# A bidirectional recurrence with slot attention on one core: its denominators get three buffers of their own, and the first four gates are taken in two steps

## The chip, the cores and the metric

The kernel runs on one core of one Trainium2 chip. A core has five engines with an instruction stream each: PE (matrix products and transposes), DVE (vector operations), ACT (activation functions from tables, copies), POOL (vector operations too) and SP, which here issues most of the DMA transfers; ACT issues some. They meet only at semaphores. The metric is the device time of one launch in microseconds, the median of several runs: 1080.36 us before the change (five runs, 1079.99 to 1083.6).

## The reference

`x` is 4 x 1024 x 1024 (batch, tokens, features), `fside` has the same shape and `cond` is 4 x 256. First a recurrence runs over the tokens, forward and backward, for each of the 4 x 1024 pairs of batch and feature on its own. `fside` is both the key and the value, `x` goes through a sigmoid as a gate:

```python
tf = sigmoid(sum(time_emb, -1))
decay = exp(-exp(w)) * (0.5 + 0.5 * tf)
ek = exp(min(k, 30.0)); ekv = ek * v
# scan over tokens: a = a * decay + ekv_t ; b = b * decay + ek_t   (forward: nf, df; reversed: nb, db)
euk = exp(min(u + k, 30.0))
num = nf + nb - ekv + euk * v
den = df + db - ek + euk
out = sigmoid(r) * (num / max(den, 1e-08)) * (0.8 + 0.2 * tf)
```

Its result passes two blocks of a slot attention: logits of each token against 16 slots, the four best tokens of each slot written into it, 16 heads of attention of all tokens over the 16 slots, an output projection and a normalisation by the root of the mean square. At the end `x` is added. All is float32.

## The kernel before

**The recurrence** takes the first 400 us or so. Features lie on the 128 partitions and tokens along them, so that one *tile* is 128 features of one batch by 1024 tokens. There are N = 32 tiles, eight per batch; the loop over `i` begins at line 587. Every four tiles share one buffer of gates (`HK` = 4).

What one tile `i` goes through, by engine:

- SP loads the keys (`kf`, four buffers) and, four tiles at a time, the gates' input (`load_gates`, L273, four transfers into one buffer of 4 x 1024 columns).
- ACT: exponentials of the keys (`terms_exp`, L292; `own_exp`, L315), the edge values that carry a forward sum into the backward scan (`make_edge`, L344, one for the denominator and one for the numerator), a matrix with the decay on its diagonal (`decay_matrix`, L382), and the first guess of the quotient, Ln and then Exp of the denominator (`guess`, L426 and L428). Also copies out of PSUM and the Square of the output (L468).
- POOL: clamping and `ekv` (`terms`, L302, L308); the floor of the denominator (L405); denominator times guess and gate times guess (`gated`, L441, L442); gate times the corrected factor (`product`, L465).
- DVE: forward scans of `ek` and `ekv`, backward scan of the denominator (`scan`, L323), the token's own term added to the denominator (`den_sum`, L352), a Newton step on the quotient (`newton`, L452), the own term of the numerator (`own_value`, L365), and the backward scan of the numerator over pairs of tokens (`numerator`, L411).
- PE: sums for the numerator (`make_pairs`, `add_pairs`), the products for the logits and sums of squares (`contract`, L476), transposes of the output rows (L493), and preparations of weights.

The order is written out by hand: `pin` (L78) keeps the instructions of each engine in the order of the program text. The tiles overlap: while tile `i` is in its scans, tile `i-1` gets its quotient and tile `i-2` its rows. In round `i` POOL's order is L441 and L442 of tile `i-1`, L302 and L308 of tile `i+1`, L405 of tile `i`, L465 of tile `i-1`. DVE's order is the two forward scans and the backward scan of tile `i`, L352 of tile `i`, L452 of tile `i-1`, L365 and L411 of tile `i`. ACT ends a round with `guess` of tile `i` and the exponential of tile `i+2`.

**The sigmoids** are taken for four tiles at once at the head of every fourth round (`gates`, L278, called at L605). The sigmoid and the pair of Exp and Ln lie in different table sets of ACT, so that each call of `gates` has a table load before it (shown at L279) and one after it (L177). Rounds with `i % HK == 0` take a branch of their own (L596 to L609): they have no transposes of rows, first PE's sums, then on ACT the Square, `own_exp`, the first edge, the sigmoids, the second edge. All other rounds take the branch from L610, with rows of tile `i-2` turned and copied between those steps.

**The buffers.** Denominator and numerator of a tile lie in one buffer, `both`, of 2 x 1024 columns and two more, of which one holds the numerator's edge. There are two such buffers, so the first write of tile `i` (the forward scan of `ek` at L323) waits until the last reader of tile `i-2` is done. For the denominator's part that is POOL's product L465, which stands at the end of round `i-1`. The other rotating buffers named below are `ek`, `ekv` and `quo`, two each. After the loop a tile `raw_sb` with a buffer of its own (tag `ov`) and `stage_last` (tag `both`) are used for the logits and the last rows.

**After the recurrence** come the two blocks, in which PE is busy nearly all the time. The change does not touch them.

Of the kernel before, what the change touches and what calls it, by code (L numbers as in the profile page):

```python
# [10 lines left out]
F32 = mybir.dt.float32  # L11
U32 = mybir.dt.uint32
AF = mybir.ActivationFunctionType
# [5 lines left out]
P = 128  # L19
# [19 lines left out]
def kernel(  # L39
# [25 lines left out]
    nc = tc.nc  # L65
# [193 lines left out]
    with rec_stack:  # L259
# [15 lines left out]
            for k in range(HK):  # L275
                move(gate[n][:, k, :], xt[n // 2, ts(n % 2 * HK + k, P), :])

        def gates(n):  # L278
            pin(nc.scalar.activation(gate[n], gate[n], AF.Sigmoid))  # L279
            pin(load_exp_ln())  # L280

        def gate_of(i):
# [44 lines left out]

        def sums(i, ek, ekv, parts):

            flat = rec.tile([P, 2 * L + 2], F32, tag="both", bufs=2, name=f"both_{i}")  # L330
            both = flat[:, : 2 * L].rearrange("p (n t) -> p n t", n=2)
            for n, src in enumerate((ek, ekv)):
                dst = both[:, n, :]
                for part in parts:
                    at = part.start
                    scan(
                        dst[:, part], src[:, part], i, dst[:, at - 1 : at] if at else 0.0, False
                    )
            return flat, both, [edges[:, i % 8, :], flat[:, 2 * L : 2 * L + 1]]

        def make_edge(i, both, edge, n):

            b, k = i // NK, i % NK
            pin(nc.scalar.mul(edge[n], both[:, n, L - 1 : L], turn[:, b, k : k + 1]))  # L344

        def denominator(i, both, edge):
            den = both[:, 0, :]
            scan(den, den, i, edge[0], True)

        def den_sum(both, own):  # L350
            den = both[:, 0, :]
            pin(nc.vector.scalar_tensor_tensor(den, own, EXP_CLAMP, den, ALU.min, ALU.add))  # L352


# [28 lines left out]
            return m  # L383

        def make_pairs(i, both, by):
            f = both[:, 1, :].rearrange("p (s h) -> p h s", h=2)
            pairs = rec_ps.tile([P, 4, P], F32, tag="ptr", bufs=1, name=f"pairs_{i}")
            pairs = pairs.rearrange("p q c -> p (q c)")
            pin(nc.tensor.matmul(pairs, by, f[:, 1], start=True, stop=False))
            pin(nc.tensor.matmul(pairs, ident, f[:, 0], start=False, stop=True))  # L390
            return pairs

        def add_pairs(num_ps, flat, by):

            f = flat[:, L : 2 * L].rearrange("p (s h) -> p h s", h=2)
            later = flat[:, L + 2 :].rearrange("p (s h) -> p h s", h=2)[:, 0]
            return [
                lambda: add(num_ps, 0, f[:, 0]),
                lambda: add(num_ps, 1, f[:, 1]),
                lambda: add(num_ps, 1, later, by),  # L400
            ]

        def floor(both):
            den = both[:, 0, :]
            pin(nc.gpsimd.tensor_scalar(den, den, DEN_MAX, DEN_MIN, ALU.min, ALU.max))  # L405

        def numerator(i, both, edge, pairs):
            even = both[:, 1, :].rearrange("p (s h) -> p h s", h=2)[:, 0]
            dec = decay_2[:, i // NK, i % NK : i % NK + 1].to_broadcast([P, L // 2])
            pin(  # L410
                nc.vector.tensor_tensor_scan(  # L411
                    even[:, ::-1], dec, pairs[:, ::-1], edge[1], ALU.mult, ALU.add
                )
            )

        def numerator_half(i, both, edge, h):

            num = both[:, 1, ts(h, 512)]
            scan(num, num, i, edge[1] if h else both[:, 1, 512:513], True)

        def guess(i, both, parts=(every,)):

            quo = rec.tile([P, L], F32, tag="quo", bufs=2, name=f"quo_{i}")
            b = i // NK
            for part in parts:
                pin(nc.scalar.activation(quo[:, part], both[:, 0, part], AF.Ln))  # L426
                pin(
                    nc.scalar.activation(  # L428
                        quo[:, part],
                        quo[:, part],  # L430
                        AF.Exp,
                        scale=-1.0,
                        bias=half_log_gain[:, b : b + 1],
                    )
                )
            return quo

        def gated(i, both, quo, part=every):
            xk = gate_of(i)[:, part]
            den = both[:, 0, part]  # L440
            pin(nc.gpsimd.tensor_tensor(den, den, quo[:, part], ALU.mult))  # L441
            pin(nc.gpsimd.tensor_tensor(xk, xk, quo[:, part], ALU.mult))  # L442

        def newton(i, both, quo, num_ps, part=every, out=None):

            b = i // NK
            den = both[:, 0, part]
            num = num_ps[:, part]
            if out is None:
                den, num = parted(den, i), by_half(num)  # L450
            pin(
                nc.vector.scalar_tensor_tensor(  # L452
                    den if out is None else out[:, part],
                    den,
                    twice_root[:, b : b + 1],
                    num,
                    ALU.subtract,
                    ALU.mult,
                    reverse0=True,
                )  # L460
            )
# [125 lines left out]
        for i in range(N):  # L587
# [5 lines left out]
            flat[i], both[i], edge[i] = sums(i, ek[i], ekv[i], [every] if past else halves)  # L593

            adds = add_pairs(num_ps[i - 1], flat[i - 1], by[i - 1]) if past else [lambda: None] * 3
            if i % HK == 0:  # L596
                for fill in adds:
                    fill()
                if older:
                    square(i - 2, quo[i - 2])  # L600
                own_exp(i, kf[i], own[i])
                make_edge(i, both[i], edge[i], 0)
                if i == 0:
                    make_edge(i, both[i], edge[i], 1)
                gates(i // HK)  # L605
                if past:
                    make_edge(i, both[i], edge[i], 1)
                    late_stage = staged(i - 2)
                    contract(i - 2, quo[i - 2], NK)  # L609
            else:  # L610
                blocks = []
                if older:
                    stage = staged(i - 2)
                    blocks = [rows_block(i - 2, h, stage) for h in range(2)]
                if i > HK and i % HK > 1:
                    blocks.append(rows_block(i - i % HK - 2, i % HK - 2, late_stage))
                if i >= 3 and projection:
                    blocks.append(projection.pop(0))
                blocks = blocks[:2] + [None] * (4 - len(blocks)) + blocks[2:]
                copy = [None] * 4  # L620

                def turn_block(n):
                    copy[n] = blocks[n]() if blocks[n] else lambda: None

                turn_block(0)
                adds[0]()
                copy[0]()
                if older:
                    square(i - 2, quo[i - 2])
                adds[1]()  # L630
                make_edge(i, both[i], edge[i], 0)
                turn_block(1)
                adds[2]()
                copy[1]()
                own_exp(i, kf[i], own[i])
                turn_block(2)
                if older:
                    contract(i - 2, quo[i - 2], NK, (0,))
                copy[2]()
                make_edge(i, both[i], edge[i], 1)  # L640
                turn_block(3)
                if older:
                    contract(i - 2, quo[i - 2], NK, (1,))
                copy[3]()
# [32 lines left out]
            floor(both[i])  # L677
            if past:
                newton(i - 1, both[i - 1], quo[i - 1], num_ps[i - 1])
                product(i - 1, both[i - 1][:, 0, :], nc.gpsimd)  # L680
                store_turned(i - 1)
            num_ps[i] = own_value(i, kf[i], own[i])
            if i == N - 1:
# [11 lines left out]

        i = N - 1
        halves = [(h, ts(h, 512)) for h in (1, 0)]
        raw_sb = rec.tile([P, L], F32, tag="ov", bufs=1, name="raw_sb")
        sq = rec_ps.tile([P, L], F32, tag="own", bufs=1, name="sq")
        eps_col = rc.tile([P, 1], F32, name="eps_col")  # L700
        nc.gpsimd.memset(eps_col, EPS)
# [7 lines left out]
        for n, (h, part) in enumerate(halves):  # L709
            numerator_half(i, both[i], edge[i], h)  # L710
            gated(i, both[i], quo[i], part)
            add(num_ps[i], h, both[i][:, 1, part])
            if n == 0:
                contract_half(i - 1, False, h)
        contract_half(i - 1, True, 1)
# [54 lines left out]
        for n in range(4):  # L770
            for q in range(4):
                block = gate_of(i - 1 + n // 2)[:, ts(4 * (n % 2) + q, P)]
                pin(nc.tensor.transpose(banks[n][:, q, :], block, ident))
        stage_last = rec.tile([P, 2 * L + 2], F32, tag="both", bufs=2, name="stage_last")[:, :L]
        stage_last = stage_last.rearrange("p (t c) -> p t c", c=P)
        for j, stage in ((i - 1, staged(i - 1)), (i, stage_last)):
            for h in range(2):
# [663 lines left out]
```

## Time and profile before

| | |
|---|---|
| median of five runs | 1080.36 us (1079.99 to 1083.6) |
| profiled execution, its own time | 1079.68 us |
| its span | 1077.3 us |
| mean granted clock of PE | 0.987 |
| busy: PE, DVE, POOL, ACT | 985.9, 739.4, 548.5, 516.2 us |
| 100 to 350 us: DVE busy in each 50 us | 48.34 to 48.83 us |
| 100 to 350 us: POOL busy in each 50 us | 48.60 to 48.94 us |
| 447 us to the end: PE busy | 613.55 of 630.30 us |

The span runs from the first to the last instruction on the core; the execution's own time has 2.4 us more around it. A busy time counts the instructions of one engine, with overlaps between two that follow each other counted once. In a row of the timeline the first number is the start in us from the span's start, the second the duration, and the brackets tell for how long the engine stood idle before and what ended that. In the chain of work the columns are start, length and what the end hung on at that time. Tile names are those of the program without numbers; `both` is the buffer of denominator and numerator.

### The profile page before, as it was taken

The numbers are of one execution on the slowest core, as the hardware profiler recorded it, in microseconds if no ns is written. First come the engines' busy times: TensorE is split into PE (matmuls) and PEld (weight loads), VectorE is DVE, ScalarE is ACT, GpSimd is POOL, SyncE is SP. The second block draws the span as 40 slices with busy tenths as digits, with TensorE's granted clock in tenths as the row PEclk, the third lists the DMA queues.
The fourth block names the chain that finished last, engine by engine and source line by source line (L and its number), as shares of the span: only waits on it lengthen the run. The fifth ranks groups of instructions, "written<-read, shape, count | busy, mean of one in ns | idle before, by whom it ended". The sixth has DMA issues, their size and how long they took to land.

```text
span 1077.3 us, 12290 instructions
## 1 busy us (share of the span) xinstructions
PE 985.9 (92%) x4232; PEld 548.1 (51%) x4232; DVE 739.4 (69%) x1049; ACT 516.2 (48%) x818; POOL 548.5 (51%) x417
## 2 busy tenths in 40 slices
PE   4688898888889888999999999998999999999996
PEld 1223333232323324665666666664575767767663
DVE  7899999999999974244666565665244555555555
ACT  6586877878687742123333444444023333333332
POOL 4999999999999961001222222222001444444344
PEclk9899999999999999999999999999999999999999
DMA  8585474758655273951777786554750555555554
GB/s 276 163 306 159 163 240 144 251 175 271 186 168 166 88 247 105 368 221 64 254 269 252 275 282 245 196 176 166 284 205 21 195 182 209 195 212 191 193 206 156
DMA packets 121790, 218.81 MB, mean 203 GB/s; under 512 B 10928, under 2 KB 76592, under 8 KB 121728
## 3 DMA queue, kind: packets, MB, share of 16 engines
q1 hardware_dynamic: 87872, 199.15, 52.6%
q10 hardware_dynamic: 33280, 16.78, 5.4%
q0 software_dynamic: 576, 2.10, 0.5%
q8 instruction: 33, 0.54, 0.2%
q14 instruction: 29, 0.24, 0.1%
HBM read 150.90 MB, written 67.11 MB: 202 GB/s over the span
## 4 chain that ended last, share of the span: by engine, by line
PE 60%; POOL 18%; ACT 9%; issue 7%; DVE 3%; DMA 1%; SPq 1%; POOLq 0%; ACTq 0%; DVEq 0%
PE psc L1170 21%; PE po L1227 19%; POOL gate L442 4%; POOL ekv L308 4%; POOL gate L465 3%; PE ptr L1158 3%; PE pk L1030 3%; PE pkv L960 3%; PE pv L1098 2%; POOL both L405 2%; POOL ek L302 2%; POOL both L441 2%; ACT quo L428 2%; ACT quo L426 1%; PE pet L1216 1%
## 5 line engine op out<-in xcount | busy, mean ns | idle before, releaser
L1170 PE MATMUL psc<-km,xt 128*128 128x272 f32 (+1 forms) x1024 | 238.4, 386 | 0.0
L1227 PE MATMUL po<-vm,e 128*128 128x512 f32 x512 | 230.4, 593 | 0.9 <-ACT e L1217 0.9
L1170 PEld LDWEIGHTS psc<-km,xt 128*128 128x128 f32 x1024 | 189.5, 190 | 29.1
L1204 POOL TENSOR_TENSOR e<-e,den 128x256 f32<-128x256 f32 x64 | 40.6, 635 | 252.4 <-DVE den L1202 231.3
L1227 PEld LDWEIGHTS po<-vm,e 128*128 128x128 f32 x512 | 94.8, 190 | 95.7 <-issue 84.9
L1268 DVE SCALAR_TENSOR_TENSOR y<-y,inv,npost_bc 128x1024 f32<-128x1024 f32 x62 | 79.6, 1284 | 41.3 <-POOL inv L1263 41.3
L1236 DVE TENSOR_TENSOR y<-po,y 128x512 f32<-128x512 f32 x128 | 85.9, 674 | 30.2 <-PE po L1227 29.9
L1256 ACT ACTIVATE junk<-y 128x1024 f32<-128x1024 f32 x63 | 66.7, 1059 | 69.3 <-DVE y L1268 69.1
L1263 POOL TENSOR_TENSOR inv<-mean,minus_half 128x1 f32<-128x1 f32 x64 | 35.6, 557 | 96.8 <-DVE mean L1261 96.8
L441 POOL TENSOR_TENSOR both<-both,quo 128x1024 f32<-128x1024 f32 (+1 forms) x33 | 77.0, 2334 | 11.0 <-ACT quo L428 9.5
L373 PE MATMUL num<-both,ident 128*128 128x512 f32 x128 | 68.8, 660 | 10.1 <-DVE both L411 6.8
L308 POOL TENSOR_TENSOR ekv<-ek,kf 128x1024 f32<-128x1024 f32 (+1 forms) x33 | 76.4, 2315 | 2.6
L1217 ACT COPY e<-pet 128x256 f32<-128x256 f32 x64 | 23.8, 372 | 112.4 <-PE pet L1216 112.3
L323 DVE TENSOR_TENSOR_SCAN both<-columns,ek 128x1024 f32<-128x1024 f32 (+1 forms) x32 | 72.2, 2255 | 7.9 <-POOL gate L465 6.5
L442 POOL TENSOR_TENSOR gate<-gate,quo 128x1024 f32<-128x1024 f32 (+1 forms) x33 | 76.2, 2308 | 0.0
L323 DVE TENSOR_TENSOR_SCAN both<-columns,edges,both 128x1024 f32<-128x1024 f32 x32 | 74.4, 2325 | 1.7 <-ACT edges L344 1.7
L1365 POOL TENSOR_TENSOR y<-y,xin 128x1024 f32<-128x1024 f32 x31 | 73.2, 2360 | 1.4 <-DVE y L1268 1.4
L465 POOL TENSOR_TENSOR gate<-gate,both 128x1024 f32<-128x1024 f32 x31 | 73.5, 2372 | 0.3
L323 DVE TENSOR_TENSOR_SCAN both<-columns,ekv 128x1024 f32<-128x1024 f32 (+1 forms) x32 | 71.4, 2231 | 0.0
L1161 ACT COPY xt<-ptr 128x512 f32<-128x512 f32 x64 | 36.9, 577 | 69.3 <-PE ptr L1158 69.3
L1261 DVE TENSOR_SCALAR mean<-total 128x1 f32<-128x1 f32 x64 | 9.8, 154 | 85.8 <-ACT junk L1256 45.8
L476 PE MATMUL raw<-quo,lhs 128*32 128x512 f32 x128 | 65.3, 602 | 0.0
(214 smaller groups left out, 1638.8 us busy)
## 6 DMA issues: line engine op xcount, KB each, us to landing
y<-rows SPq DMA_DIRECT2D x64, 512.0 KB, 4.3
kf<-in_ft_dram SPq DMA_DIRECT2D x32, 512.0 KB, 5.2
gate<-in_xt_dram SPq DMA_DIRECT2D x32, 512.0 KB, 7.6
turned_rows<-gate SPq DMA_DIRECT2D x32, 512.0 KB, 3.5
xt<-turned_rows SPq DMA_DIRECT2D x32, 512.0 KB, 5.6
rows<-y SPq DMA_DIRECT2D x32, 512.0 KB, 3.0
xin<-in_x_dram SPq DMA_DIRECT2D x32, 512.0 KB, 4.6
rows<-stage ACTq DMA_DIRECT2D x31, 512.0 KB, 3.7
```

What stands on the lines that cost most here:

```text
L308: pin(nc.gpsimd.tensor_tensor(ekv[:, part], ek[:, part], kf[:, part], ALU.mult))
L323: nc.vector.tensor_tensor_scan(dst[:, way], dec, src[:, way], start, ALU.mult, ALU.add)
L373: nc.tensor.matmul(num_ps[:, ts(h, 512)], by, src, start=False, stop=True, skip_group_check=True)
L441: pin(nc.gpsimd.tensor_tensor(den, den, quo[:, part], ALU.mult))
L442: pin(nc.gpsimd.tensor_tensor(xk, xk, quo[:, part], ALU.mult))
L465: pin(engine.tensor_tensor(xk, xk, factor[:, part], ALU.mult))
L1170: nc.tensor.matmul(psc[g][:, :n], xt_g[g][:, k, :], maps["km"][:, g // NT, k, :n], start=(k == 0), stop=(k == NK - 1),)
L1227: nc.tensor.matmul(po, et[:, ts(c, P)], vm[:, c, ts(h, 512)], start=(c == 0), stop=(c == 1),)
L1236: pin(nc.vector.tensor_add(half, po, half))
L1256: pin(nc.scalar.activation(junk, src, AF.Square, accum_out=total))
L1268: pin(nc.vector.scalar_tensor_tensor(y[g], y[g], inv[g], npost_bc, ALU.mult, ALU.mult))
L1365: pin(nc.gpsimd.tensor_add(y[g - 1], y[g - 1], xin[g - 1]))
```

## The change

It has three parts.

1. Each denominator gets a buffer of its own, `den`, of which there are three. The numerator and its edge stay in a buffer `num_sb` of 1024 + 2 columns, two of them. `both` becomes a list of the two, and the functions that took a slice of the old tile take an element of the list.
2. `gates` is called with the tile's number. At tile 0 it takes the sigmoid of feature tile 0 only, at tile 1 that of the feature tiles 1 to 3; at tiles 4, 8, ... that of all four as before. Tile 1 therefore takes the branch that the fourth tiles take; the square and the contraction in it are now only done where there is a tile `i-2`.
3. `raw_sb` moves into a buffer of `ekv`, and `stage_last` into one of `num_sb`. The space of the old `ov` buffer (1024 columns) goes into the third denominator.

```diff
-        def gates(n):
-            pin(nc.scalar.activation(gate[n], gate[n], AF.Sigmoid))
+        def gates(i):
+            part = gate[i // HK]
+            if i < 2:
+                part = part[:, i : i + 1 + 2 * i, :]
+            pin(nc.scalar.activation(part, part, AF.Sigmoid))
             pin(load_exp_ln())
...
         def sums(i, ek, ekv, parts):
-            flat = rec.tile([P, 2 * L + 2], F32, tag="both", bufs=2, name=f"both_{i}")
-            both = flat[:, : 2 * L].rearrange("p (n t) -> p n t", n=2)
+            den = rec.tile([P, L], F32, tag="den", bufs=3, name=f"den_{i}")
+            flat = rec.tile([P, L + 2], F32, tag="num_sb", bufs=2, name=f"num_sb_{i}")
+            both = [den, flat[:, :L]]
             for n, src in enumerate((ek, ekv)):
-                dst = both[:, n, :]
+                dst = both[n]
...
-            return flat, both, [edges[:, i % 8, :], flat[:, 2 * L : 2 * L + 1]]
+            return flat, both, [edges[:, i % 8, :], flat[:, L : L + 1]]
...
-            if i % HK == 0:
+            if i % HK == 0 or i == 1:
                 for fill in adds:
                     fill()
                 if older:
...
                 make_edge(i, both[i], edge[i], 0)
                 if i == 0:
                     make_edge(i, both[i], edge[i], 1)
-                gates(i // HK)
+                gates(i)
                 if past:
                     make_edge(i, both[i], edge[i], 1)
+                if older:
                     late_stage = staged(i - 2)
                     contract(i - 2, quo[i - 2], NK)
...
-        raw_sb = rec.tile([P, L], F32, tag="ov", bufs=1, name="raw_sb")
+        raw_sb = rec.tile([P, L], F32, tag="ekv", bufs=2, name="raw_sb")
...
-        stage_last = rec.tile([P, 2 * L + 2], F32, tag="both", bufs=2, name="stage_last")[:, :L]
+        stage_last = rec.tile([P, L + 2], F32, tag="num_sb", bufs=2, name="stage_last")[:, :L]
```

The other lines of the change replace `both[:, 0, :]` by `both[0]`, `both[:, 1, :]` by `both[1]`, and the offsets into `flat` that went with them.

More of the change, by code (lines that the diff above doesn't have):

```diff
@@ L338, in sums @@
                     )
-            return flat, both, [edges[:, i % 8, :], flat[:, 2 * L : 2 * L + 1]]
+            return flat, both, [edges[:, i % 8, :], flat[:, L : L + 1]]
         def make_edge(i, both, edge, n):
             b, k = i // NK, i % NK
-            pin(nc.scalar.mul(edge[n], both[:, n, L - 1 : L], turn[:, b, k : k + 1]))
+            pin(nc.scalar.mul(edge[n], both[n][:, L - 1 : L], turn[:, b, k : k + 1]))
         def denominator(i, both, edge):
-            den = both[:, 0, :]
+            den = both[0]
             scan(den, den, i, edge[0], True)
         def den_sum(both, own):
-            den = both[:, 0, :]
+            den = both[0]
             pin(nc.vector.scalar_tensor_tensor(den, own, EXP_CLAMP, den, ALU.min, ALU.add))
@@ L385, in make_pairs @@
         def make_pairs(i, both, by):
-            f = both[:, 1, :].rearrange("p (s h) -> p h s", h=2)
+            f = both[1].rearrange("p (s h) -> p h s", h=2)
             pairs = rec_ps.tile([P, 4, P], F32, tag="ptr", bufs=1, name=f"pairs_{i}")
@@ L393, in add_pairs @@
         def add_pairs(num_ps, flat, by):
-            f = flat[:, L : 2 * L].rearrange("p (s h) -> p h s", h=2)
-            later = flat[:, L + 2 :].rearrange("p (s h) -> p h s", h=2)[:, 0]
+            f = flat[:, :L].rearrange("p (s h) -> p h s", h=2)
+            later = flat[:, 2:].rearrange("p (s h) -> p h s", h=2)[:, 0]
             return [
@@ L403, in floor @@
         def floor(both):
-            den = both[:, 0, :]
+            den = both[0]
             pin(nc.gpsimd.tensor_scalar(den, den, DEN_MAX, DEN_MIN, ALU.min, ALU.max))
         def numerator(i, both, edge, pairs):
-            even = both[:, 1, :].rearrange("p (s h) -> p h s", h=2)[:, 0]
+            even = both[1].rearrange("p (s h) -> p h s", h=2)[:, 0]
             dec = decay_2[:, i // NK, i % NK : i % NK + 1].to_broadcast([P, L // 2])
@@ L416, in numerator_half @@
         def numerator_half(i, both, edge, h):
-            num = both[:, 1, ts(h, 512)]
-            scan(num, num, i, edge[1] if h else both[:, 1, 512:513], True)
+            num = both[1][:, ts(h, 512)]
+            scan(num, num, i, edge[1] if h else both[1][:, 512:513], True)
         def guess(i, both, parts=(every,)):
@@ L425, in guess @@
             for part in parts:
-                pin(nc.scalar.activation(quo[:, part], both[:, 0, part], AF.Ln))
+                pin(nc.scalar.activation(quo[:, part], both[0][:, part], AF.Ln))
                 pin(
@@ L439, in gated @@
             xk = gate_of(i)[:, part]
-            den = both[:, 0, part]
+            den = both[0][:, part]
             pin(nc.gpsimd.tensor_tensor(den, den, quo[:, part], ALU.mult))
@@ L446, in newton @@
             b = i // NK
-            den = both[:, 0, part]
+            den = both[0][:, part]
             num = num_ps[:, part]
@@ L679 @@
                 newton(i - 1, both[i - 1], quo[i - 1], num_ps[i - 1])
-                product(i - 1, both[i - 1][:, 0, :], nc.gpsimd)
+                product(i - 1, both[i - 1][0], nc.gpsimd)
                 store_turned(i - 1)
@@ L711 @@
             gated(i, both[i], quo[i], part)
-            add(num_ps[i], h, both[i][:, 1, part])
+            add(num_ps[i], h, both[i][1][:, part])
             if n == 0:
```

## The prediction

> **What bounds the kernel now.** I read the page first, then the waits of POOL and DVE in the recurrence (18 to 400 us), then the chain of work in order of time over its first 135 us, and last the timeline around the first tiles and around one later group. From the page:
>
> ```profile
> span 1077.3 us, 12290 instructions
> PE 985.9 (92%) x4232; PEld 548.1 (51%) x4232; DVE 739.4 (69%) x1049; ACT 516.2 (48%) x818; POOL 548.5 (51%) x417
> DVE  7899999999999974244666565665244555555555
> POOL 4999999999999961001222222222001444444344
> ```
>
> One slice is 27 us. PE leads the whole span, but the change touches only the first 15 slices, and there POOL and DVE stand at 9 together. In a steady round POOL starts L441 at 85.54 and again at 97.27: 11.73 us, with no idle time between its six operations. So in the recurrence the end is set by POOL, and what POOL waits for is what can be won:
>
> ```profile
> POOL both L441 <- ACT quo L428: 9.5, 8, 6.1
> POOL both L405 <- DVE both L352: 6.5, 4, 3.6
> DVE both L323 <- POOL gate L465: 6.5, 8, 3.2
> ```
>
> Columns: total us, times, longest. POOL waits 9.5 us for the guess of the quotient, 6.1 of them once. L405 waits 2.2 us in tile 0, 0.5 in tile 2, 0.2 in tile 14 and 3.6 in the last tile. The third row is the wait that the third denominator buffer takes away: the forward scan waits for the product of two tiles before. The longest wait of POOL, followed back by the chain (start, us, what):
>
> ```profile
> 10.62 6.52 DMA gate<-in_xt_dram
> ...
> 17.19 1.28 ACT L279
> ...
> 18.48 3.62 ACT gate L279
> ...
> 22.12 1.28 ACT L177
> ...
> 23.41 0.40 ACT decay_matrix L382
> 23.82 0.95 ACT quo L426
> ...
> 24.80 1.16 ACT quo L428
> ```
>
> The fourth load of gate tiles ends it: ACT then loads a table, takes the sigmoid of four feature tiles, loads the old table, and only then comes to the guess of tile 0. The input of that guess had been there since 20.01, as the timeline shows (last two rows: one later group):
>
> ```profile
> 15.34 0.29 ACT L344 ACTIVATE both<-both,turn 128x1 f32<-128x1 f32 x1 [2.21 <-DVE both L323]
> 18.97 1.04 POOL L405 TENSOR_SCALAR both<-both 128x1024 f32<-128x1024 f32 x1 [2.22 <-DVE both L352]
> 26.09 2.38 POOL L441 TENSOR_TENSOR both<-both,quo 128x1024 f32<-128x1024 f32 x1 [6.08 <-ACT quo L428]
> 35.36 1.06 ACT L426 ACTIVATE quo<-both 128x1024 f32<-128x1024 f32 x1 [6.67 <-POOL both L405]
> 37.68 2.29 DVE L323 TENSOR_TENSOR_SCAN both<-columns,ek 128x1024 f32<-128x1024 f32 x1 [3.16 <-POOL gate L465]
> 117.03 1.28 ACT L177 ACT_TABLE_LOAD   x1
> 118.32 0.29 ACT L344 ACTIVATE both<-both,turn 128x1 f32<-128x1 f32 x1
> ```
>
> **Part 1: beside tile 0 one sigmoid instead of four.** It needs the first gate load only. The four loads are 512 KB each, and the DMA view moves about 410 GB/s from 14 to 20 us, so 1.28 us each; the last is in at about 17.14, the first therefore at about 17.14 - 3 x 1.28 = 13.3. (Were nothing in order between them, 17.14: that is a rival below.) ACT is free after the edges at 15.34 + 0.29 = 15.63. From there: table load 1.28 to 16.92; one tile of 1024 columns 1.06 (the Square of L468, same shape, 1.06) to 17.98; table back 1.28 to 19.27; decay matrix 0.39 to 19.66. The floor of tile 0 ends at 18.97 + 1.04 = 20.01, set by DVE and not by ACT. So Ln starts at 20.05 instead of 23.72: **3.67 us earlier**. Exp follows, and L441 starts at about 22.4 instead of 26.09. POOL's wait of 6.08 falls to 2.4, and what is late next is the floor itself, behind L352 on DVE.
>
> **Part 2: beside tile 1 the other three.** The table is loaded two times more: 2 x 1.28 on ACT. Three tiles cost 2.77 us by the line between 1.06 for one and 3.62 for four; bounds 2.56 (3.62 - 1.06) and 3.62. The branch for tile 1 also puts own_exp ahead of the first edge, and the sigmoids ahead of the second. ACT in the new order: Ln and Exp of tile 0 to 22.3; ek of tile 2 to 23.3; own_exp (1.10) to 24.4; edge 0 to 24.6; table to 25.9; three sigmoids to 28.7 (29.5 at the upper bound); table to 30.0 (30.8); edge 1 to 30.2 (31.1); decay matrix to 30.5 (31.4). Who waits for each:
> - DVE's backward scan of the denominator needs edge 0 at 24.6. The forward scans of tile 1 end at 23.22 + 2.26 = 25.48, so it starts there, not at 27.20 as now: the 1.72 us that DVE waited for the edge go.
> - DVE's numerator scan needs edge 1. DVE reaches it at 25.4 + 2.3 (scan) + 1.15 (L352) + 1.25 (L452) + 1.15 (L365) = 31.3, so 0.2 to 1.1 us of cover are left.
> - The next guess waits for the floor of tile 1. POOL goes L441, L442, L302, L308, L405 from 22.4, in the 9.2 us that 26.09 to 35.29 shows, so the floor ends at 31.6; ACT is free at 30.5 (31.4). It starts at 31.67 instead of 35.36: again 3.69 us earlier.
> - POOL's L442 of tile 1, the first that reads a gate of the other three, comes at about 36.4, 7 us after they are done.
>
> So the 6.2 us of ACT work moved into tile 1 lie in a stretch in which ACT is idle now: 6.67 us before 35.36. Cost on the path: 0, up to 0.1 at the upper bound. If that cover were gone, every us of ACT beyond 1.1 would be a us of POOL.
>
> **Part 3: a third denominator buffer, numerators apart.** No instruction is added on DVE, POOL, PE or SP; the scan of ek no longer waits for the product of tile i-2. Those 6.5 us of DVE wait are not on POOL's path, except where L405 waits for DVE. That is tile 2, 0.50 us at 46.45, and there L352 waits for own_exp on ACT (0.67), behind a copy from PE, behind transposes of tile 0's product, all on a slow clock (granted 0.50 from 32.5 to 42). That runs from the product, not from the scan: it moves with POOL and stays. Later, DVE's own round is 11.6 us and POOL's 11.73, so DVE can only run ahead, until it meets the edge (edge 0 is there at 99.84, the scan takes it at 101.62) or own_exp (102.37 and 104.04): 1.7 us at most. In every fourth tile POOL's 0.53 us before L441 (121.18) follow floor, ACT's row of work and two table loads, none of which the buffer moves. In tile 30, DVE's L411 at 380.78 waits for PE's pairs, which follow the product of tile 28. Worth: taken as 0; bounds -0.5 (tile 2's stall goes) and +1.2 (below).
>
> **Part 4: raw_sb in an ekv buffer, stage_last in a numerator buffer.** Both old readers are scans of tiles 30 and 31 long done when DVE copies raw at 403.81: 0. SP's queue has the same loads and stores in the same order; the store of tile 0 and all behind it go 3.7 us earlier with the product.
>
> **Sum.** -3.67 (part 1), 0 to +0.1 (part 2), 0 (-0.5 to +1.2; parts 3 and 4): -3.7 us. All later stages hang on the recurrence's end, so the profiled execution goes from 1079.68 (span 1077.3) to 1076.0. That execution lies 0.68 below the median of the runs, 1080.36, so for the median I say **1076.7**, 0.34% faster. Under 0.2%, 2.2 us, no measurement of this kernel tells a change from none.
>
> **The switch of tables, weighed.** It costs 1.28 us each way in the rows above: the load at 117.03 ends at 118.31 and the next activation starts at 118.32, with nothing between. The Trainium skill, page "ScalarE: Activation LUTs", section "What ACT_TABLE_LOAD costs", gives about 2.66 us for every switch to another set, 1.28 for the load and 1.38 for a drain, and the page's rule is to batch calls by set, which speaks against a second pair of switches. By that rule the sum would be about 0 and the time about 1080.6 (an estimate from the page's figure), which is rival 2; here the trace disagrees, since no drain stands behind the load at 117.03.
>
> **Rivals.**
> 1. *Forecast*, 0.78: 1074.9 to 1078.2.
> 2. *No change: a switch holds ACT for longer than its row.* If each of the four took d longer, ACT would come to the guess of tile 0 at 19.66 + 2d, past the floor from d = 0.2 on, and to that of tile 1 at 30.1 + 4d; POOL's L441 of tile 1 follows 2.4 us later, now at 37.74. The gain is gone at d = 1.3, when a switch takes twice its row: 1080.0 to 1080.7. Against it: 117.03, and the same at 69.67, where the edge follows at 70.96. 0.04.
> 3. *The change does not do what it says:* the first sigmoid still waits for all four loads, because they fill one tile. Then ACT starts its table at 17.19, the guess at 21.2, and 2.5 us are won: 1077.9. Against it: the four are separate transfers into separate parts. In the same class I put a small loss on POOL (up to the +1.2 of part 3) and one in tile 1. Together 0.13, at 1077.9 to 1079.3, half of it over the 0.2% line.
> 4. *Slower:* DVE, no longer tied to the product, meets other POOL operations, and both read the same memory. POOL's long operations show 2.34 to 2.41 us; if all four of a round went up by that spread of 0.07, 29 rounds would cost 8.1 us and the time would be 1084.8. It decides from 51 ns for each, (3.7 + 2.2)/(29 x 4). Against it: the lead is at most 1.7 us of 11.73, so that 15% of the meetings change (8.1 x 0.15 = 1.2 us, the bound of part 3), and L441 takes 2.38 at 26.09 with DVE idle. 0.05.
>
> **The numbers.** Faster 0.78 + 0.07 = 0.85; within 0.2% 0.04 + 0.06 = 0.10; slower 0.05. The range 1074.9 to 1078.6 takes the forecast with its bounds and part of case 3.
>
> **What would show it.** L441 of tile 0 starts near 22.4 with about 2.4 us of wait; four table loads before 31 us; the Ln of tile 1 near 31.7; the wait of L441 for the guess in total 5.8 us instead of 9.5; the scan's wait for the product gone, DVE no faster at the end; POOL's round still 11.73; the last product about 3.7 us earlier. I am wrong if the first Ln starts after 21, if ACT is still at sigmoids when the floor of tile 1 ends, or if POOL's round is longer than 11.8.

## The result, and the profile after

The changed kernel's median is 1078.81 us (36 runs), that of the kernel before, in the same comparison, 1082.07 us (62 runs). The ratio is 0.9966, 95% interval 0.9955 to 0.9976: 0.34% faster, 3.7 us of 1080. (The means, 1078.62 and 1082.33, lie 3.7 us apart as well, the medians 3.3.) The predicted 1076.7 was counted from 1080.36, the median of the first five runs, which lay low; 0.9966 x 1080.36 = 1076.7. Taken as it stands, 1078.81 is 0.2 us over the upper end of the stated range.

The page of the changed kernel:

```profile
span 1077.1 us, 12278 instructions
PE 990.4 (92%) x4232; PEld 550.5 (51%) x4232; DVE 737.5 (68%) x1049; ACT 518.0 (48%) x821; POOL 548.0 (51%) x417
DVE  8999999999999963244656565665244555555555
POOL 6999999999999951001222222222001444444344
```

POOL's row shows both ends of the gain: its first digit rose from 4 to 6, and the fifteenth fell from 6 to 5, since the recurrence ends earlier. Yet this profiled execution (1078.88, span 1077.1) is only 0.2 us shorter in span than the one before. Both are true: 4.0 us were won before 400 us, and 3.8 lost again behind them. First the gain. The waits of POOL and of DVE from 16 to 400 us (total us, times, longest):

```profile
POOL den L447 <- ACT quo L434: 5.9, 8, 2.4
POOL den L411 <- DVE den L358: 5.9, 3, 3.5
...
DVE den L358 <- ACT own L320: 3.7, 3, 1.9
DVE num_sb L417 <- PE pairs L396: 2.7, 3, 1.7
```

The lines have moved by six (L441 is L447 now, L405 is L411, L323 is L328, L465 is L471). POOL's wait for the guess fell from 9.5 to 5.9 us, the longest from 6.1 to 2.4. DVE's scan waits for no product any more; DVE waits for ACT and for PE in its place. The timeline shows the two steps of the sigmoids:

```profile
15.63 1.28 ACT L284 ACT_TABLE_LOAD   x1
16.92 1.06 ACT L284 ACTIVATE gate<-gate 128x1024 f32<-128x1024 f32 x1
18.00 1.28 ACT L177 ACT_TABLE_LOAD   x1
20.02 1.06 ACT L432 ACTIVATE quo<-den 128x1024 f32<-128x1024 f32 x1 [0.33 <-POOL den L411]
22.40 2.36 POOL L447 TENSOR_TENSOR den<-den,quo 128x1024 f32<-128x1024 f32 x1 [2.42 <-ACT quo L434]
25.83 2.77 ACT L284 ACTIVATE gate<-gate 128x3072 f32<-128x3072 f32 x1
31.72 1.06 ACT L432 ACTIVATE quo<-den 128x1024 f32<-128x1024 f32 x1 [1.22 <-POOL den L411]
393.32 1.26 POOL L448 TENSOR_TENSOR gate<-gate,quo 128x512 f32<-128x512 f32 x1
```

ACT now waits for the floor (0.33 and 1.22 us in the brackets), where the floor of tile 0 lay ready and waited for ACT before. The last POOL operation of the recurrence, the last row above, ends at 394.58, in the kernel before at 398.59. Its end is called the end of POOL's last product below. Of these 4.0 us, 3.7 are the earlier first product (22.40 instead of 26.09). Most of the rest is POOL's wait at tile 2, which fell from 0.50 to 0.22 us.

Then the loss. Behind the search for the best tokens, the first block gathers rows and multiplies them (tiles `pmix` and `pw`, on PE). The same stage in the profiled execution of the changed kernel, and after it of the kernel before; columns: stretch, its length, busy us and instructions of PE, PEld (PE's weight loads), DVE, ACT, POOL, then the granted clock as a share of the full one, the DMA share and GB/s:

```profile
420.20:436.10 15.90, 13.90 (x65) 7.35 (x64) 1.56 (x3) 0.37 (x1) 0.90 (x2) 0.79 0.37 129
```

```profile
424.20:436.30 12.10, 10.84 (x64) 5.86 (x64) 1.60 (x3) 0.37 (x1) 0.88 (x1) 1.00 0.42 138
```

Nothing in this stage was changed. It took 3.8 us longer for two reasons. `pmix` started 0.8 us later behind the issue of the gather (5.9 us instead of 5.1), since the rows came later. And the clock granted to PE was halved in part of the stage (0.79 as a mean), which is the other 3.0 us: `pmix` took 4.86 us instead of 3.76, `pw` 9.02 instead of 7.09. PE's `pmix`, in the changed kernel and in the kernel before:

```profile
421.70 4.86 PE L899 MATMUL pmix<-spare,spare 128*128 128x64 f32 x32 [1.48 <-POOL bias_rows L890]
```

```profile
424.89 3.76 PE L892 MATMUL pmix<-spare,spare 128*128 128x64 f32 x32 [0.69 <-issue]
```

(The engine in the brackets of `pmix` is not what ended the wait: in the kernel before `pmix` starts while POOL still works on `bias_rows`.) So one profile against one profile says "no change" where 98 runs say 0.34%.

### The profile page after: what moved, and what is told of

Same layout as the page of the kernel before. It is cut to its first block, busy times and chain, and to the rows that moved or that the text cites. A ratio compares the mean times of both kernels' runs of the same rounds, so it can differ in the third digit from the quotient of the medians.

```text
span 1077.1 us, 12278 instructions
## 1 busy us (share of the span) xinstructions
PE 990.4 (92%) x4232; PEld 550.5 (51%) x4232; DVE 737.5 (68%) x1049; ACT 518.0 (48%) x821; POOL 548.0 (51%) x417
## 4 chain that ended last, share of the span: by engine, by line
PE 60%; POOL 19%; ACT 7%; issue 7%; DVE 6%; DMA 1%; POOLq 0%; DVEq 0%; SPq 0%; ACTq 0%
PE psc L1177 21%; PE po L1234 19%; POOL gate L448 4%; POOL ekv L313 4%; POOL gate L471 3%; PE ptr L1165 3%; PE pk L1037 3%; PE pkv L967 3%; PE pv L1105 2%; POOL ek L307 2%; POOL den L411 2%; POOL den L447 2%; DVE den L328 2%; ACT quo L434 2%; PE pw L917 1%
## 5 line engine op out<-in xcount | busy, mean ns | idle before, releaser
L447 POOL TENSOR_TENSOR den<-den,quo 128x1024 f32<-128x1024 f32 (+1 forms) x33 | 77.1, 2336 | 7.8 <-ACT quo L434 5.9
L379 PE MATMUL num<-num_sb,ident 128*128 128x512 f32 x128 | 70.8, 677 | 6.6 <-DVE num_sb L417 3.3
L328 DVE TENSOR_TENSOR_SCAN den<-columns,edges,den 128x1024 f32<-128x1024 f32 x32 | 74.4, 2326 | 0.0
L471 POOL TENSOR_TENSOR gate<-gate,den 128x1024 f32<-128x1024 f32 x31 | 73.3, 2365 | 0.3 <-DVE den L458 0.2
L328 DVE TENSOR_TENSOR_SCAN den<-columns,ek 128x1024 f32<-128x1024 f32 (+1 forms) x32 | 71.4, 2232 | 0.0
L328 DVE TENSOR_TENSOR_SCAN num_sb<-columns,ekv 128x1024 f32<-128x1024 f32 (+1 forms) x32 | 71.4, 2231 | 0.0
```

The costliest lines, as they stand in the source:

```text
L328: nc.vector.tensor_tensor_scan(dst[:, way], dec, src[:, way], start, ALU.mult, ALU.add)
L379: nc.tensor.matmul(num_ps[:, ts(h, 512)], by, src, start=False, stop=True, skip_group_check=True)
L471: pin(engine.tensor_tensor(xk, xk, factor[:, part], ALU.mult))
```

## The experiments

Executions start their first tile up to 0.9 us apart, so the recurrence is best compared from the start of the first floor (L405 or L411 of tile 0) to the end of POOL's last product. All in us, each from one profiled execution:

| kernel | first floor | first L441 (L447) | last product ends | from floor | median |
|---|---|---|---|---|---|
| before | 18.97 | 26.09 | 398.59 | 379.62 | 1082.07 |
| changed | 18.95 | 22.40 | 394.58 | 375.63 | 1078.81 |
| 1: sigmoids only | 18.82 | 22.28 | 394.59 | 375.77 | 1078.97 |
| 2: buffers only | 19.61 | 25.81 | 398.41 | 378.80 | 1082.94 |
| 3: three squares more | 18.83 | 22.29 | 396.52 | 377.69 | 1079.44 |
| 4: decay matrix later | 19.47 | 22.93 | 394.02 | 374.55 | 1076.36 |
| 5: changed, with holds | 19.69 | 23.15 | 395.50 | 375.81 | 1078.40 |
| 6: before, with holds | 19.48 | 26.36 | 401.41 | 381.93 | 1081.76 |
| 7: 4 with holds and an earlier block | 19.68 | 23.14 | 392.88 | 373.20 | 1074.03 |

The medians of 1 to 4 stand beside 1082.42 for the kernel before, on one chip; those of 5 to 7 beside 1082.86, on another.

### 1. The sigmoids alone

The kernel before, with the new `gates`, the branch for tile 1 and nothing else:

```diff
-            if i % HK == 0:
+            if i % HK == 0 or i == 1:
...
-                gates(i // HK)
+                gates(i)
```

> The kernel before with the split of the first sigmoids alone (one tile beside tile 0, three beside tile 1, and tile 1 on the branch of the fourth tiles); denominator and numerator stay in one buffer, of which there are two. Theory: the gain is all in the split. POOL's first product of denominator and guess starts at 22.4 instead of 26.09, the last POOL product of the recurrence ends about 3.7 us before 398.59, the time is 3.5 to 4.0 us under the kernel before. The forward scan of tile 2 waits for the product of tile 0, some 1 to 2 us, and the scan's other waits stay; none of them moves POOL. Rival: the split needs the third buffer, because DVE, kept back by the product, becomes late for POOL once POOL starts earlier; then the last product comes 0.3 to 2 us later than in the full change.

The ratio to the kernel before is 0.9959 (0.9943 to 0.9975). From the floor, the recurrence takes 375.77 us, 0.14 more than with the full change. The waits of this kernel, where L470 is the product:

```profile
POOL both L446 <- ACT quo L433: 5.8, 8, 2.4
...
DVE both L328 <- POOL gate L470: 4.6, 8, 1.4
```

DVE still waits eight times for the product, and POOL is as early as with three buffers. The theory holds: the split is the whole gain as far as these runs tell, and the rival's 0.3 to 2 us are 0.14. Even that is within what PE's clock moves: in this execution the floors of tiles 15, 19 and 26 wait 0.78 us together, some 20 us behind the starts of stretches of half clock, and in the changed kernel's they don't.

### 2. The buffers alone

The full change with the old `gates` and the old condition:

```diff
-            if i % HK == 0 or i == 1:
+            if i % HK == 0:
...
-                gates(i)
+                gates(i // HK)
```

> The full change without its split: three denominator buffers, raw_sb and the last stage moved, but four sigmoids beside tile 0 as before. Theory: the scan's 6.5 us of waits for the product go, and nothing else: POOL's first product at 26.1, the last one within 0.5 us of 398.59, the time within 0.5 us of the kernel before. Rival: the earlier scans win about 0.3 us at tile 2 and at the end each, so that the last product comes 0.5 to 1 us before 398.59.

0.9997 (0.9980 to 1.0014). The waits:

```profile
POOL den L442 <- ACT quo L429: 8.6, 8, 5.2
POOL den L406 <- DVE den L353: 6.5, 4, 3.5
...
DVE den L353 <- ACT own L315: 5.2, 4, 2.2
```

The scan's row for the product is gone, 6.5 us of waits, and nothing came of it: DVE waits 5.2 us for `own_exp` instead of 0.7. The 0.8 us that this recurrence is shorter from the floor lie wholly ahead of the first product: the first tile started 0.64 us late, while the gates' load, which sets that product here, did not. From the first product to the end of the last it takes 372.60 us, the kernel before 372.50.

### 3. How much cover tile 1 has

```diff
                 gates(i)
                 if past:
                     make_edge(i, both[i], edge[i], 1)
+                if i == 1:
+                    spare = rec.tile([P, L], F32, tag="late_stage", bufs=1, name="spare_act")
+                    for _ in range(3):
+                        pin(nc.scalar.activation(spare, kf[i], AF.Square))
```

> The full change with three more ACT operations of 1.06 us in tile 1, behind the second edge (Square of the keys into a spare tile, read by nobody). In the changed kernel ACT then stood idle for 1.22 us before the guess of tile 1. Theory: that is all the cover the move has, so of 3.2 to 3.3 us about 2.0 us come through to POOL, and stay: POOL's product of tile 1 starts at 36.1 instead of 34.10, the last one about 2.0 us later than 394.58. Rival: POOL has slack of its own behind it (it stalls at tile 2 and in every fourth tile), so less than 1 us is left at the end.

The timeline of this kernel:

```profile
30.00 3.22 ACT L617 ACTIVATE spare_act<-kf 128x1024 f32<-128x1024 f32 x3
33.41 1.04 ACT L432 ACTIVATE quo<-den 128x1024 f32<-128x1024 f32 x1
35.78 2.38 POOL L447 TENSOR_TENSOR den<-den,quo 128x1024 f32<-128x1024 f32 x1 [1.91 <-ACT quo L434]
```

Of 3.2 us put into ACT, 1.2 vanish in the cover, and POOL waits for the rest: counted from the first floor, its product of tile 1 comes 1.8 us later than in the changed kernel (35.78 instead of 34.10, with the floor 0.12 earlier). The recurrence takes 377.69 us, 2.06 more. The last 0.3 us are not the squares': in this execution POOL waits 0.55 us for the floor's input at tile 5, behind a stretch of half clock (70.2 to 77.1 us), and not at tile 2. Nothing behind tile 1 gives the 1.8 us back. So the cover that the prediction worked out for the guess of tile 1 (31.6 against 30.5, 1.1 us) is real, and it is all there is. The ratio to the kernel before, 0.9974 (0.9960 to 0.9987), is what is left of the gain.

### 4. The wait in every fourth tile

POOL's remaining waits for the guess are one in each fourth tile, where ACT works without a pause from the floor of one tile to the guess of the next. One operation of that row is not needed in it:

```diff
-            if i + 1 < N - 1:
+            if i + 1 < N - 1 and (i % HK or not i):
                 by[i + 1] = decay_matrix(i + 1)
...
             quo[i] = guess(i, both[i])
+            if i and i % HK == 0:
+                by[i + 1] = decay_matrix(i + 1)
```

> The full change, and in tiles 4, 8, ..., 28 the decay matrix of the next tile is made behind the guess instead of ahead of it. Theory: POOL's wait in every fourth tile (0.53 to 0.56 us, the first 0.2) ends with ACT's row of work from floor to guess, in which the decay matrix takes 0.29 us from start to start; each of six waits falls by 0.29 and the first to 0, so POOL's wait for the guess falls from 5.9 to about 4.0 us, the last product comes about 1.9 us before 394.58. Rival: the wait is set by something else that ends at the same time (the second edge, or DVE), and the last product stays within 0.4 us of 394.58.

```profile
POOL den L411 <- DVE den L358: 6.8, 3, 4.1
POOL den L447 <- ACT quo L434: 4.0, 7, 2.4
```

The waits for the guess fell as expected, 5.9 to 4.0 us; the recurrence only by 1.08 us. The row above says where the rest went: the floor's wait for DVE. Two of its three places (the third is tile 0, as before), in the timeline:

```profile
361.35 1.04 POOL L411 TENSOR_SCALAR den<-den 128x1024 f32<-128x1024 f32 x1 [0.46 <-DVE den L358]
385.52 1.04 POOL L411 TENSOR_SCALAR den<-den 128x1024 f32<-128x1024 f32 x1 [4.08 <-DVE den L358]
```

0.46 us are at tile 29, where PE's clock was halved (351.6 to 358.4 us), and 0.6 at the last tile, where POOL waits 4.08 instead of 3.47: POOL is earlier, the tail is not. On the other side the 0.22 us at tile 2 are gone. The theory was right on the wait and short on its worth. Ratio 0.9944 (0.9928 to 0.9961).

### 5 and 6. What halves the clock, and the change without it

Sorted, the 36 times of the changed kernel have a gap between 1077.35 and 1078.52. In both kernels more filler products were put on PE in the two stages behind the token searches:

```diff
-        hold_clock(bank("po", f"idle_rows{blk}"), 5 if first else 1)
+        hold_clock(bank("po", f"idle_rows{blk}"), 7 if first else 1)
...
         pin(nc.vector.tensor_copy(token, compact(at, "token")))
+        if last:
+            hold_clock(bank("po", "idle_token"), 2)
```

> The full change with more filler products on PE in the two stages behind the token searches: 7 instead of 5 before the gathered rows come in the first block, and 2 between the two small products of the second block, where PE stood idle for about 2 us in all. Theory: the changed kernel's executions fall in two groups, 1075.0 to 1077.4 and 1078.5 to 1082.9, because in some of them PE's clock is halved in one of these two stages (424.12 to 430.95 us in the profiled one, where the products for the mix and the write took 13.9 us instead of 10.9). With PE kept busy the second group goes: all executions between 1075.0 and 1078.5, and the median is 1 to 2.5 us below that of the changed kernel, since the fillers themselves cost 0.3 to 1.1 us. Rival: the groups come from elsewhere, and executions above 1079 stay as frequent.

> The kernel before with the same fillers. Theory: its slow group goes too, its executions lie within 3 us of each other around 1080, and the changed kernel with fillers is 3.5 to 4.2 us faster than it, which is the change measured without the clock's share. Rival: part of the 0.34% came from the clock and the difference is below 3 us.

In both profiled executions the two stages ran at full clock, and so they did in that of experiment 7. In the six without more fillers the clock was halved in the first block's stage three times and in the second block's each time. The stage of the first block in the changed kernel with fillers:

```profile
422.66:433.90 11.24, 10.77 (x65) 5.75 (x63) 1.55 (x2) 0.37 (x1) 0.00 (x0) 1.00 0.36 116
```

The executions lie closer, 1076.92 to 1080.43 and 1080.74 to 1084.21, 3.5 us from first to last in each (12 runs), where the changed kernel had 7.9 (36 runs, and the kernel before 6.4 in 23 on the chip of 5 and 6). But the expectation was wrong in its other half: the lowest times rose, from 1075.0 to 1076.9, in the kernel before from 1078.73 to 1080.74, the ratio to the kernel before stayed, 0.9967 (0.9952 to 0.9981), and 3 of 12 executions are still above 1079 (16 of 36 without more fillers). Put into the kernel before, the fillers alone give 0.9991 (0.9979 to 1.0004), no change that these runs can tell. They cost about what they save. In all three profiled executions with them they held PE until `pmix`, which started 5.9 us behind the issue of the gather; in the six without it was 5.0 to 5.9. In that of 5 the clock was also halved at a third place, 476.4 to 479.8 us. The two stages are one source of the spread, not the only one; what sets the others is open.

What the pair does show is the change with about half of that spread taken from both sides: 1078.40 against 1081.76, 3.4 us. That is a little under the 3.5 to 4.2 expected and above the rival's 3; twelve runs a side, each 3.5 us wide, do not tell 3.4 from 3.7. In the main the gain is thus no gift of the clock. The runs of 6 lie around 1082, not around 1080. Its profile is the slowest of them (1084.21). Its recurrence takes 381.93 us because PE is at half clock more often: behind four such stretches (from 180.7, 228.5, 276.3 and 324.1 us on) the floors of tiles 14, 19, 23 and 27 wait 1.8 us together, and behind a fifth, from 378.7 us on, the last floor waits 4.86 us instead of 3.61.

### 7. The tail

In tile 30 of the changed kernel DVE's numerator scan waits 1.66 us for PE, which has the last block of weight preparation there (0.68 us in experiment 4). One block more in tile 9 moves all later ones up by a place:

```diff
                 if i >= 3 and projection:
                     blocks.append(projection.pop(0))
+                if i == 9:
+                    blocks.append(projection.pop(0))
```

with the edits of 4 and the fillers of 5.

> The full change with the fillers, the decay matrix of every fourth tile behind the guess, and one more block of weight preparation in tile 9, so that the last one (16 small products, 1.96 us on PE) falls in tile 29, which has no late rows to turn, instead of tile 30. Theory: with the matrix moved, only 1.1 of 1.9 us came through, because in tile 30 DVE's numerator scan waits for PE (1.66 us in the changed kernel) and the tail hangs on that; with the block gone from tile 30 that wait goes, the last product ends 1.2 to 2 us earlier than the 371.1 us behind POOL's first product that it took with the matrix alone, and the time is 2 to 3.5 us under the changed kernel with fillers. Rival: PE is late in tile 29 instead and the tail stays where it is, within 0.5 us.

```profile
373.92 1.23 DVE L371 SCALAR_TENSOR_TENSOR num<-own,kf 128x1024 f32<-128x1024 f32 x1
375.06 1.27 DVE L417 TENSOR_TENSOR_SCAN num_sb<-decay,num_sb,pairs 128x512 f32<-128x512 f32 x1
...
384.35 1.04 POOL L411 TENSOR_SCALAR den<-den 128x1024 f32<-128x1024 f32 x1 [2.46 <-DVE den L358]
```

The first two rows are DVE's, in tile 30: the scan follows at once. POOL's last wait for the floor falls from 4.08 to 2.46, and the recurrence takes 1.35 us less than in 4, within the 1.2 to 2 expected. (Each of the two has waits of its own behind half clock: 0.46 us at tile 29 in 4, 0.68 at tiles 25 and 26 here.) The median is 1074.03, the ratio 0.9929 (0.9906 to 0.9952): 0.7% under the kernel before. Against the changed kernel with fillers it is 4.4 us less, where 2 to 3.5 were expected and the two recurrences differ by 2.6; with six runs here, whether the rest is more than spread is open. This may be where the third buffer counts. With two buffers the forward scan of tile 31, which starts at 376.25 here, would have to wait for the product of tile 29, which ends at 377.05: 0.8 us, an estimate from this trace. The version was not tried with two.

## Why the prediction was right, and where it was off

- **Part 1**, 3.67 us earlier: the guess of tile 0 starts at 20.02 instead of 23.72 (20.05 was forecast), L447 at 22.40. The first of four loads held nothing up: ACT starts its table load at 15.63 without a wait, where the kernel before waited 1.56 us for the gates. So the rival by which the first sigmoid waits for all four falls.
- **Part 2**, cost 0: every forecast start lies within 0.1 us. The three sigmoids took 2.77 us, the interpolated value; edge 1 was done at 30.20 and the guess of tile 1 started at 31.72. The "6.2 us of ACT work" take the upper bound for the sigmoids; the stretch took 5.4 us (24.54 to 29.90). Experiment 3 shows the cover, 1.2 us, against 1.1 worked out.
- **Part 3**, taken as 0 within -0.5 to +1.2: experiment 2 measures 0.1 the wrong way, experiment 1 against the full change 0.14 the right way; neither is more than the clock moves in a recurrence. One reading was wrong: tile 2's wait was to move with POOL and stay, and it fell from 0.50 to 0.22. The buffers are not the cause, for it is 0.52 in experiment 2 and gone in experiment 1. It goes with the end of the half clock there, counted from the start of the first product: 16.6 us behind it in experiment 2, 16.3 in the kernel before, 16.0 in the changed kernel, and no wait where it is 15.4 or less (1, 4, 6 and 7). These 0.3 us are thus luck of the profiled execution. The row that looked largest in favour of the buffers, 6.5 us of DVE waits, was off the path throughout. POOL's round stayed at 11.7 us, so the rival of slower POOL operations falls. (Its counter-argument held only in part: while L441 took 2.38 us at 26.09, DVE was idle for the first 1.1 us of it.)
- **The switch of tables:** the 2.66 us of the Trainium skill's page "ScalarE: Activation LUTs" (section "What ACT_TABLE_LOAD costs") do not hold here: the load at 15.63 ends at 16.91 and the sigmoid starts at 16.92, in the kernel where rival 2 would have shown. So that rival falls too.
- **The sum**, -3.7: the recurrence became 4.0 us shorter, 0.3 of it at tile 2 and owed to the clock; the runs give 3.7 (0.34%).
- **What was mis-sized** is the last step, from the recurrence to the span: "all later stages hang on the recurrence's end" is right for the median and not for one execution. The forecast of 1076.0 for the profiled execution missed by 2.9 us, since 3.8 us went to one stage that no edit touches, 3.0 of them to the clock and 0.8 to the gathered rows. The range had no term for that, although the five runs shown already reached from 1079.99 to 1083.6. Nor was it seen that a median of five runs with such a spread can lie 1.7 us below that of 62.

## What to carry to other kernels

Split an operation that waits for several loads when only its first part is on the path, and put the rest where the engine stands idle; count that idle stretch first, because what exceeds it comes through in full (3.2 us put in, 1.2 covered, POOL 1.8 later). A wait removed from an engine that is not the bound buys nothing by itself (6.5 us of it moved the end by 0.1, no more than the clock does). For effects of some tenths of a per cent, compare the stage in the profile from a common event and the runs by their ratio, never two spans.

## What the runs showed of the hardware

PE's granted clock changes on a grid of 3.41 us, which lies differently in each execution: in the nine traces the halved stretches before the last one are 3.41, 6.83, 10.24 or 17.07 us long. In the changed kernel's profile the clock fell at 424.12, after a step of the grid in which PE had stood idle for 1.0 us (420.71 to 421.70) and then ran the small products of `pmix`; in the kernel before a step with 0.5 us of idle time left it alone. Idle time alone does not decide it, though: in experiment 1 the clock stayed up behind a step with 0.94 us of it (421.35 to 422.29), and in experiment 3 it fell at 428.63 behind a step with 0.45 us (427.97 to 428.42), the rest of which was nearly all `pmix`. What the rule is stays open. In experiment 1 the clock fell in the second block, for 17.07 us from 747.09 on, and `pmix` and `pw` took 6.93 and 9.79 us instead of 3.76 and 7.09: 5.9 us, more than the change is worth.
